# Four of 32 row tiles get their vector added by TensorE instead of VectorE, two inverse roots go to GpSimd, thirteen instead of fourteen places for x, and a new order of the work

## The chip, the cores and the metric

The kernel runs on one core of one Trainium2 chip. The metric is the device time of one execution in microseconds (us): the median of three runs of the kernel before is 146.02 us (145.58 to 146.04). Engines are named as in the profile: PE is TensorE, DVE is VectorE, ACT is ScalarE, POOL is GpSimd, SP is SyncE, which here only issues DMAs. Sequences carry a q (SPq, ACTq): the time in which such an engine issues a DMA.

## The reference

x has 8 sequences of 512 rows of 1024 float32 values, 16 MB. Each sequence is cut into 8 blocks of rows, and one vector p per sequence is made from them and added to all its rows; what follows is a layer norm and a residual.

```python
block_repr = inputs.reshape(B, 8, block_size, H).sum(axis=2)
keys = einsum('bnh,kh->bnk', block_repr, Wk)
keys = keys / sqrt(mean(keys * keys, -1) + EPS) * rms_weight
attn = softmax(einsum('bnh,h->bn', keys, cond[1]))
attended = einsum('bn,bnh->bh', attn, block_repr)
p = einsum('bsh,kh->bsk', attended, Wo)       # the same for all rows of a sequence
y = x + p
out = x + (y - mean(y)) / sqrt(var(y) + EPS) * ln_gamma + ln_beta
```

## The kernel before

**Tiles and groups.** The 8 sequences are three groups of 2, 4 and 2 sequences (`GROUPS`). A "row" is a tile of 128 partitions by 1024 values; there are 32 rows, 0 to 7 in group 0, 8 to 23 in group 1, 24 to 31 in group 2. A load of 1 MB brings two rows: x0.0 is rows 0 and 1, x1.2 is rows 12 and 13, x1.3 rows 14 and 15, x2.3 rows 30 and 31. Loaded tiles live in 14 places of SBUF (`XSLOTS`), in which the 8 MB of the two weight matrices also stand before they are transposed. A result is written over its row in place, stored from there, and only then can the place take another load.

**A group's p.** PE sums the blocks (bs, L429), DVE turns the sums into columns (col, L439), PE multiplies by Wk (proj.0, L473), then comes the softmax: ACT squares (L496), DVE sums keys by q (qk, L498), PE collects both (L505), DVE forms the mean square cv (L507), and an inverse root of it is made by `inverse_root`: ACT takes logarithm and exponential (L484, L485), and three small steps n1, n2, n3 on DVE or POOL (L486 to L489) refine it. After scores, maximum, exponential (L513) and sum (wc, L516), PE multiplies by Wo (proj.1), DVE or ACT weighs that (vw, L529 or L530), PE spreads it over 128 partitions (L545), and two copies make `pb`, p of the group in SBUF. Four small DMAs (tb, L387) put p's rows into a table `tab` that also holds gamma and beta.

**A row k** is worked on in five steps, whose labels are used below:

- S_k (DVE, L646): x = x + p in place, with the row's sum beside it
- Q_k (ACT, L648): the sum of squares around the mean
- D_k (DVE, L746): (gamma + std) * x into a pair of PSUM banks
- R_k (PE, L732): outer products that add what depends on the row's statistics, for two rows in one go
- E_k (ACT, L761): PSUM times 1 / std back into the row, which is then stored (L813)

Rows form units of 2 or 4 (`UNITS`); a unit's statistics are worked on by POOL (s2, v, std, sd2, rs; std and rs are powers of 0.5 and -0.5, L695 and L715), transposed by PE (L721) and copied out of PSUM (lt, L241 on ACT or L243 on DVE). D, R and E share three pairs of PSUM banks, so D of a row waits for E of a row three places earlier.

**The order** is written out by hand: `Plan` collects the steps with what they read and write, and `ORDER` lists their numbers in the order in which they are given to the engines (with the bank or place that a step takes, and a letter for the engine where there is a choice). Each engine works through its own part of that list strictly in order. Words such as `f1:7` are matmuls with zeros, which open a bank for accumulation and keep PE at work.

`UKIND` names the way of each unit. In kind `c` the steps are as above. Kind `p`, which is in the code before but used by no unit, leaves x as it is: B_k sums the row, Bp sums p (both independent of each other), POOL adds the two sums (`totals`), Y_k on PE adds x (times an identity) and p in PSUM, and Q_k squares from there. Its outer products then take p * gamma from a second table, `tabx`.

## Time and profile before

| | us |
|---|---|
| median of three runs | 146.02 |
| time of the profiled execution | 144.9 |
| its span, first to last instruction | 143.2 |
| DVE busy in the span | 95.5 |
| ACT busy | 90.9 |
| PE busy (zeros among it) | 112.3 |
| POOL busy | 58.5 |

The second part of the page cuts the span in 40 slices. DMA is at 9 tenths or more in slices 1 to 15, up to about 57 us: the loads of the weights and of most of x. From slice 20 on DVE shows 9 in nearly each slice, and ACT 8 or 9: there the rows are worked on. Of 42.76 MB, 25.73 are read and 16.78 written; 1 MB of a load takes some 2.5 us when the DMA engines are full. The granted clock of TensorE is 0.932 on average.

### The profile page before, as it was taken

Reading aid. Unit: us, or ns where it says so; the run is one execution under the profiler, and the core shown is the slowest. Engines: PE = TensorE matmul, PEld = TensorE weight load, DVE = VectorE, ACT = ScalarE, POOL = GpSimd, SP = SyncE. Lnnn points to the kernel's source line nnn. Section 1 sums busy time; section 2 is a strip of 40 time slices with the busy share of each in tenths; the row PEclk is TensorE's granted clock in tenths of the full one; section 3 lists DMA queues with packets and bytes.
Section 4 is the critical chain, followed back from the end, with each engine's and each line's share of the span. In section 5 each row is a group of like instructions: output and inputs, shape, how many; then the busy total and the mean of one; then the engine's idle time right before and its main releaser. Section 6 shows DMA issues by size and latency. Waiting matters only on the chain.

```text
span 143.2 us, 2871 instructions
## 1 busy us (share of the span) xinstructions
PE 112.3 (78%) x1093; PEld 58.9 (41%) x1101; DVE 95.5 (67%) x161; ACT 90.9 (64%) x140; POOL 58.5 (41%) x107
## 2 busy tenths in 40 slices
...
GB/s 126 427 413 422 413 409 414 410 411 423 426 410 424 410 413 420 263 0 238 204 307 417 314 295 5 293 89 204 291 298 6 347 240 0 295 293 220 411 401 145
DMA packets 7526, 42.76 MB, mean 299 GB/s; under 512 B 808, under 2 KB 808, under 8 KB 3672
## 3 DMA queue, kind: packets, MB, share of 16 engines
...
HBM read 25.73 MB, written 16.78 MB: 297 GB/s over the span
## 4 chain that ended last, share of the span: by engine, by line
DMA 33%; PE 24%; DVE 17%; ACT 11%; issue 6%; POOL 3%; SPq 2%; DVEq 0%; ACTq 0%
PE b L473 11%; DVE t L746 9%; DMA gam<-in_L_cond_ln_gamma_dram 8%; DMA x<-in_L_cond_Wo_dram 8%; DMA x<-in_L_cond_Wk_dram 6%; DMA x<-in_x_dram 5%; PE t L732 5%; PE t L407 4%; ACT x L761 4%; DVE x L646 4%; ACT square L648 3%; DMA tab<-in_L_cond_ln_gamma_dram 3%; DMA pb<-in_cond_dram 3%; ACT woT L241 2%; PE b L429 1%
## 5 line engine op out<-in xcount | busy, mean ns | idle before, releaser
L746 DVE SCALAR_TENSOR_TENSOR t<-gam,ustd,x 128x1024 f32<-128x1024 f32 x31 | 39.1, 1291 | 3.7 <-ACT x L761 2.5
L648 ACT ACTIVATE square<-x,tot 128x1024 bf16<-128x1024 f32 x32 | 36.7, 1147 | 3.3 <-DVE x L646 2.1
L646 DVE SCALAR_TENSOR_TENSOR x<-x,pb 128x1024 f32<-128x1024 f32 x32 | 37.6, 1223 | 0.1
L761 ACT ACTIVATE x<-t,urs 128x1024 f32<-128x1024 f32 x31 | 33.2, 1107 | 5.5 <-PE t L732 2.4
L700 POOL TENSOR_SCALAR stat<-tot 128x8 f32<-128x8 f32 (+1 forms) x8 | 7.5, 934 | 53.1 <-DVE x L646 53.0
L732 PE MATMUL t<-tab,lt 32*128 32x512 f32 x124 | 24.9, 667 | 4.8 <-DVE lt L243 2.2
L407 PE MATMUL t<-ident,x 128*128 128x128 f32 x120 | 17.9, 316 | 5.3 <-DMA x<-in_L_cond_Wk_dram 3.0
L869 PE MATMUL b<-zeros 128*128 128x512 bf16 (+1 forms) x57 | 18.2, 439 | 2.1 <-DVE zeros L294 1.0
L407 PEld LDWEIGHTS t<-ident,x 128*128 128x128 f32 x120 | 16.9, 202 | 6.6 <-issue 4.7
L869 PEld LDWEIGHTS <-zeros 128*128 128x128 bf16 x87 | 8.7, 108 | 17.2 <-issue 12.8
L695 POOL TENSOR_TENSOR ustd<-uv,halfs 128x4 f32<-128x4 f32 (+1 forms) x8 | 13.3, 1660 | 5.5 <-DVE uv L692 4.1
L732 PEld LDWEIGHTS t<-tab,lt 32*128 32x128 f32 x124 | 7.5, 191 | 16.9 <-DVE t L746 5.7
L241 ACT COPY wkT<-t 128x1024 f32<-128x1024 f32 x5 | 5.1, 1013 | 14.1 <-PE t L407 14.1
L715 POOL TENSOR_TENSOR urs<-uv,halfs 128x4 f32<-128x4 f32 (+1 forms) x8 | 13.2, 1650 | 0.0
L243 DVE COPY wkT<-t 128x1024 f32<-128x1024 f32 x3 | 3.7, 1225 | 12.1 <-PE t L407 12.1
L429 PE MATMUL b<-x,blk 128*32 128x256 f32 x128 | 8.4, 384 | 4.2 <-DMA x<-in_x_dram 3.7
L473 PE MATMUL b<-wkT,blkT 128*32 128x256 f32 x192 | 11.0, 380 | 0.6 <-DVE blkT L439 0.6
L241 ACT COPY woT<-t 128x1024 f32<-128x1024 f32 x6 | 5.8, 1014 | 7.8 <-PE t L407 7.8
L429 PE MATMUL t<-x,blk 128*32 128x256 f32 x128 | 7.9, 382 | 3.1 <-DMA x<-in_x_dram 3.1
L473 PEld LDWEIGHTS b<-wkT,blkT 128*32 128x32 f32 x192 | 5.9, 110 | 5.8 <-issue 1.2
L473 PE MATMUL b<-woT,blkT 128*32 128x256 f32 x128 | 7.9, 382 | 0.0
L869 PE MATMUL t<-zeros 128*128 128x512 bf16 x22 | 6.4, 380 | 1.1 <-ACT lt L241 0.6
...
## 6 DMA issues: line engine op xcount, KB each, us to landing
...
```

Of the source, the lines that this page charges most:

```text
L241: nc.scalar.copy(dst, src)
L407: nc.tensor.transpose(half(part, c // 4)[:, bass.ts(c % 4, P)], tile_of(name)[:, e % RT, c::HC], ident)
L429: nc.tensor.matmul(bank(f"bs{n}")[32 * j : 32 * j + 32, :QU], blk[G["g"]], tile_of(name)[:, r, bass.ts(j, QU)], start=(t == 0 and r == 0), ...
L473: nc.tensor.matmul(bank(name)[32 * j : 32 * j + 32, :QU], b[:, c, :], w[:, c, j], start=(c == 0), stop=(c == HC - 1),)
L646: add(f"S{k}", [(DVE, 1.15)], lambda e: nc.vector.scalar_tensor_tensor(x_row(k), x_row(k), 1.0, pb[n], ALU.mult, ALU.add, accum_out=total) ...
L648: add(f"Q{k}", [(ACT, 1.28)], lambda e: nc.scalar.activation(square, x_row(k), AF.Square, bias=total, scale=-float(H), accum_out=ssq), rea ...
L695: add(f"{T} std", [(POOL, 0.5 + 0.16 * U)], lambda e: nc.gpsimd.tensor_tensor(std, v, halfs[:, :1].to_broadcast([P, U]), ALU.pow), reads=[ ...
L715: add(f"{T} rs", [(POOL, 0.5 + 0.16 * U)], lambda e: nc.gpsimd.tensor_tensor(rs, v, halfs[:, 1:].to_broadcast([P, U]), ALU.pow), reads=[V, ...
L732: nc.tensor.matmul(half(f"row{k}", h), lts[q % NST][lo : lo + 32, r // RT, :], tab_of(k)[0][lo : lo + 32, :], start=False, stop=True, skip ...
L746: add(f"D{k}", [(DVE, 1.21)], lambda e: nc.vector.scalar_tensor_tensor(flat(pair(name)), gam, std, x_row(k), ALU.add, ALU.mult), reads=["g ...
L761: add(f"E{k}", [(ACT, 1.13)], lambda e: nc.scalar.activation(x_row(k), flat(pair(name)), AF.Identity, scale=rs), reads=[RS], writes=[xk(k) ...
L869: nc.tensor.matmul(bank_at(i)[:, :n], zeros, zeros[:, 0:1].to_broadcast([P, n]), start=start, stop=True, skip_group_check=True)
```

## The change

- Unit 3 (rows 12 to 15) becomes kind `p`: S12 to S15 on DVE go; B12, B13 and B14 on DVE and B15 on ACT sum x, Bp1.0 on DVE sums p of group 1, Y12 to Y15 are done on PE, and Q12 to Q15 read PSUM. POOL gets two steps more for the unit (`to`, and `sn`, the unit's constant columns). The table `tabx` (tx1, one DVE product) and the tile `gx` for it (four small loads by ACT) are new.
- In the softmaxes of groups 1 and 2 (`ROOT_POW`) one power on POOL takes the place of logarithm, exponential, n1, n2 and n3.
- The two tables take SBUF, so `XSLOTS` is 13; `diag` and `kw` share the tile `vw0`, and some small tiles that no kind uses are left out. The second to fourth loads of group 2 instead of the third and fourth wait for a stored place.
- `ORDER` is new in all parts. Engines of single steps change with it: the copies lt of units 2, 3, 4 and 7, vw of group 1 and one copy of its pb go from ACT to DVE; the two half scalings of the last row (E31), the copy qw and some copies of transposed weights go from DVE to ACT (one of the latter the other way); the step v of units 7 and 8 leaves DVE for POOL and ACT. 87 matmuls with zeros become 64.

```diff
-XSLOTS = 14
+XSLOTS = 13
-UKIND = 'ccccccccc'
-TABS = ((0, 'y'), (1, 'y'), (2, 'y'))
-FORMS = ('y',)
+UKIND = 'cccpccccc'
+TABS = ((0, 'y'), (1, 'x'), (1, 'y'), (2, 'y'))
+FORMS = ('x', 'y')
+ROOT_POW = (1, 2)
...
-    "42 94b 43 f1:1 119:4 44 45 46 47 72:7 106 48 120a 117:0 49 50 51 52 118a 121:2 53 54 55 56 73:8 102 57 122b "
+    "40 41 42 94a 43 f1:1 124:4 44 45 46 47 72:7 99 48 125a 122:0 49 50 51 52 123b 126:2 53 54 55 56 73:8 102 57 "
...
-    diag = alloc("diag", [P, 32])
+    diag = vw[0][:, :32]
-    kw = alloc("kw", [P, QU], BF16) if junk is None else junk[:, :QU]
+    kw = vw[0]
...
-        inverse_root(T, cv, c0, ca, ca, ("cv", "c0", "ca", "ca"))
+        if n in ROOT_POW:
+            add(f"{T} pow", [(POOL, 2.0)], lambda e: nc.gpsimd.tensor_tensor(
+                ca, cv, halfs[:, 1:].to_broadcast([P, NBLK]), ALU.pow), reads=["cv", "halfs"], writes=["ca"])
+        else:
+            inverse_root(T, cv, c0, ca, ca, ("cv", "c0", "ca", "ca"))
...
-        elif kind_of(k) == "p":
-            add(f"B{k}", [(ACT, 1.28)], lambda e: nc.scalar.activation(square, x_row(k), AF.Identity, accum_out=usx[u][:, r : r + 1]),
+        elif kind_of(k) in "pa":
+            sx = usx[u][:, r : r + 1]
+            add(f"B{k}", [(ACT, 1.34), (DVE, 1.2)], lambda e: nc.scalar.activation(
+                square, x_row(k), AF.Identity, accum_out=sx) if e == ACT else nc.vector.tensor_reduce(sx, x_row(k), AX.X, ALU.add),
                 reads=[xk(k)], writes=[f"usx{u}.{r}"])
...
+            add(f"Bp{n}.0", [(ACT, 1.34), (DVE, 1.2)], lambda e: nc.scalar.activation(
+                square, pb[n % NPB], AF.Identity, accum_out=t[:, 0:1]) if e == ACT else nc.vector.tensor_reduce(
+                t[:, 0:1], pb[n % NPB], AX.X, ALU.add),
```

The step that carries the addition, in the code before and after alike (in `moments`, kind `p`):

```python
for h in range(2):
    nc.tensor.matmul(pair(y)[:, h, :]..., ident, bands(x_row(k))[:, :, h, :], start=True, stop=False)
spread_p(G, y, False)          # four matmuls of 256 columns that add p
```

**First place: DVE around p of group 0.** L516 or L531 is the last small step of the softmax (wc), L530 or L545 is vw, the copy to `pb` ends the making of p, and then the S steps of rows 0 to 7 follow; the whole-row loads of gamma (`gam`) and col of group 1 come behind them. Before:

```order
L515 RECIPROCAL es<-es 128x1
L516 SCALAR_TENSOR_TENSOR kw,wcol<-cs,es,diag_90 128x8
L530 TENSOR_SCALAR vw_107<-t_79,wcol 128x256
L243 COPY pb_108<-b_82 128x4x128
L646 SCALAR_TENSOR_TENSOR x_64,tot_97<-x_64,pb_108 128x1024 x2
```

and now (L617 are B12 and B13, then B14):

```order
L531 SCALAR_TENSOR_TENSOR vw_105,wcol<-cs,es,diag_88 128x8
L617 TENSOR_REDUCE usx_141<-x_65 128x1 x2
L545 TENSOR_SCALAR vw_105<-t_79,wcol 128x256
L617 TENSOR_REDUCE usx_141<-x_66 128x1
L253 COPY pb_106<-b_81 128x4x128
L693 SCALAR_TENSOR_TENSOR x_64,tot_95<-x_64,pb_106 128x1024 x2
```

Two sums of x stand ahead of vw and one ahead of the copy.

**Second place: DVE between p of group 1 and col of group 2.** Before, eight S (rows 8 to 15), D8, D9, col:

```order
L646 SCALAR_TENSOR_TENSOR x_75,tot_97<-x_75,pb_109 128x1024 x2
L646 SCALAR_TENSOR_TENSOR x_76,tot_97<-x_76,pb_109 128x1024 x2
L646 SCALAR_TENSOR_TENSOR x_63,tot_98<-x_63,pb_109 128x1024 x2
L646 SCALAR_TENSOR_TENSOR x_65,tot_98<-x_65,pb_109 128x1024 x2
L746 SCALAR_TENSOR_TENSOR t_81<-gam,ustd_156,x_75 128x1024
L746 SCALAR_TENSOR_TENSOR t_79<-gam,ustd_156,x_75 128x1024
L439 STREAM_TRANSPOSE blkT_105<-b_82 128x256
```

and now four S of rows 8 to 11 with Bp1.0 (L627) among them, D7 behind them, five S of rows 16 to 20, D8, D9, the copy lt of unit 2, tx1 (L401) and col:

```order
L693 SCALAR_TENSOR_TENSOR x_75,tot_95<-x_75,pb_107 128x1024 x2
L627 TENSOR_REDUCE pmv_114<-pb_107 128x1
L693 SCALAR_TENSOR_TENSOR x_63,tot_95<-x_63,pb_107 128x1024 x2
L799 SCALAR_TENSOR_TENSOR t_78<-gam,ustd_143,x_71 128x1024
L693 SCALAR_TENSOR_TENSOR x_68,tot_95<-x_68,pb_107 128x1024 x2
L693 SCALAR_TENSOR_TENSOR x_70,tot_95<-x_70,pb_107 128x1024 x2
L693 SCALAR_TENSOR_TENSOR x_73,tot_96<-x_73,pb_107 128x1024
L799 SCALAR_TENSOR_TENSOR t_78<-gam,ustd_144,x_75 128x1024
L799 SCALAR_TENSOR_TENSOR t_80<-gam,ustd_144,x_75 128x1024
L253 COPY lt_101<-b_82 128x256
L401 TENSOR_TENSOR tabx<-tab_109,gx 128x512
L449 STREAM_TRANSPOSE blkT_103<-b_81 128x256
```

D7 was ahead of the first S of this group, and later rows' S have moved up into the place of S12 to S15.

**Third place: PE behind p of group 1.** Before, it does two block sums of group 2, R of rows 6 and 7, and the third block sum:

```order
L545 MATMUL b_83<-vw_107,spread_94 128x4x64
L869 LDWEIGHTS zeros
L869 MATMUL t_79<-zeros 128x512
L429 MATMUL b_82<-x_72,blk_91 32x256 x8
L429 MATMUL b_82<-x_74,blk_91 32x256 x8
L732 MATMUL t_79<-tab_110,lt_104 128x512 x2
L732 MATMUL t_80<-tab_110,lt_104 128x512 x2
L429 MATMUL b_82<-x_64,blk_91 32x256 x8
```

and now Y14 and Y12 (each L657 and the four L560 behind it) come first, Y15 and Y13 behind R of rows 6 and 7, and the last two block sums of group 2 after those:

```order
L657 MATMUL t_78<-x_66,ident 128x512 x2
L560 MATMUL t_78<-vw_105,spread_92 128x4x64 x4
L657 MATMUL t_80<-x_65,ident 128x512 x2
L560 MATMUL t_80<-vw_105,spread_92 128x4x64 x4
L439 MATMUL b_81<-x_74,blk_89 32x256 x8
L439 MATMUL b_81<-x_64,blk_89 32x256 x8
L785 MATMUL t_79<-tab_108,lt_102 128x512 x2
L785 MATMUL t_78<-tab_108,lt_102 128x512 x2
L657 MATMUL t_80<-x_66,ident 128x512 x2
L560 MATMUL t_80<-vw_105,spread_92 128x4x64 x4
L657 MATMUL t_79<-x_65,ident 128x512 x2
L560 MATMUL t_79<-vw_105,spread_92 128x4x64 x4
```

Behind the last row follow the transposes of unit 2, two block sums and R of rows 8 and 9. The Y steps use the pairs of banks that D, R and E share.

## Rows read from the trace of the kernel before

**Rows 1.** Windows: length; busy PE, PEld, DVE, ACT, POOL; PE clock; DMA share, GB/s.

```profile
56.14:73.64 17.50, 15.72 (x191) 7.29 (x194) 12.88 (x23) 9.97 (x20) 5.31 (x5) 1.00 0.54 200
73.64:106.62 32.98, 28.20 (x271) 12.44 (x265) 32.46 (x54) 30.64 (x49) 17.58 (x17) 0.95 0.62 252
79.00:85.00 6.00, 5.42 (x38) 1.82 (x29) 6.00 (x10) 5.55 (x9) 5.28 (x6) 0.72 0.82 327
```

**Rows 2.** Timeline of DVE, 40 to 58 us: start, length, instruction [idle before].

```profile
40.32 0.23 DVE L516 SCALAR_TENSOR_TENSOR kw<-cs,es,diag 128x8 bf16<-128x8 f32 x1
...
43.06 0.48 DVE L530 TENSOR_SCALAR vw<-t,wcol 128x256 f32<-128x256 f32 x1 [2.51 <-PE t L459]
...
45.74 1.23 DVE L646 SCALAR_TENSOR_TENSOR x<-x,pb 128x1024 f32<-128x1024 f32 x1
...
56.14 0.69 DVE L352 TENSOR_SCALAR gam<-gam 128x1024 f32<-128x1024 f32 x1 [1.10 <-DMA gam<-in_L_cond_ln_gamma_dram]
...
57.11 1.25 DVE L746 SCALAR_TENSOR_TENSOR t<-gam,ustd,x 128x1024 f32<-128x1024 f32 x1
```

**Rows 3.** Timeline of PE, 39 to 55 us.

```profile
39.30 3.70 PE L459 MATMUL t<-woT,blkT 128*32 128x192 f32 x128
...
52.36 1.07 PE L429 MATMUL t<-x,blk 128*32 128x256 f32 x16 [0.66 <-DMA x<-in_x_dram]
...
54.88 0.42 PE L429 MATMUL t<-x,blk 128*32 128x256 f32 x4 [1.13 <-DMA x<-in_x_dram]
```

**Rows 4.** Timelines of DVE, 65 to 74 us, and ACT, 72 to 74 us.

```profile
65.39 0.16 DVE L507 TENSOR_SCALAR cv<-b 128x8 f32<-128x8 f32 x1
...
67.31 0.17 DVE L489 SCALAR_TENSOR_TENSOR ca<-ca,c 128x8 f32<-128x8 f32 x1
...
72.44 1.29 DVE L746 SCALAR_TENSOR_TENSOR t<-gam,ustd,x 128x1024 f32<-128x1024 f32 x1 [0.89 <-ACT x L761]
73.64 1.22 DVE L646 SCALAR_TENSOR_TENSOR x<-x,pb 128x1024 f32<-128x1024 f32 x1
...
72.30 1.06 ACT L241 COPY pb<-b 128x512 f32<-128x512 f32 x2
```

**Rows 5.** Timeline of DVE, 111 to 117 us.

```profile
111.85 1.22 DVE L646 SCALAR_TENSOR_TENSOR x<-x,pb 128x1024 f32<-128x1024 f32 x1
...
113.00 3.69 DVE L746 SCALAR_TENSOR_TENSOR t<-gam,ustd,x 128x1024 f32<-128x1024 f32 x3
116.58 1.22 DVE L646 SCALAR_TENSOR_TENSOR x<-x,pb 128x1024 f32<-128x1024 f32 x1
```

**Rows 6.** Groups of instructions by line: busy us, mean ns, idle before.

```profile
L243 DVE COPY lt<-b 128x256 f32<-128x256 f32 x2 | 0.8, 422 | 0.0
```

**Rows 7.** Timeline of PE, 58 to 80 us.

```profile
58.20 3.66 PE L473 MATMUL b<-wkT,blkT 128*32 128x256 f32 x64
...
78.43 1.07 PE L429 MATMUL b<-x,blk 128*32 128x256 f32 x16 [2.49 <-DMA x<-in_x_dram]
```

**Rows 8.** Timeline of POOL, 52 to 53 and 110 to 112 us.

```profile
52.54 1.04 POOL L695 TENSOR_TENSOR ustd<-uv,halfs 128x4 f32<-128x4 f32 x1 [0.88 <-ACT uv L691]
...
110.92 1.91 POOL L695 TENSOR_TENSOR ustd<-uv,halfs 128x4 f32<-128x4 f32 x1
```

**Rows 9.** Timeline of ACT, 74 to 77 us.

```profile
74.90 1.15 ACT L648 ACTIVATE square<-x,tot 128x1024 bf16<-128x1024 f32 x1 [0.52 <-DVE x L646]
...
76.17 1.15 ACT L648 ACTIVATE square<-x,tot 128x1024 bf16<-128x1024 f32 x1
```

**Rows 10.** Timelines of DVE, ACT and SP, 134 to 139 us.

```profile
134.36 1.42 DVE L771 SCALAR_TENSOR_TENSOR b<-gam,ustd,x 128x512 f32<-128x512 f32 x2
136.33 1.41 DVE L780 TENSOR_SCALAR x<-b,urs 128x512 f32<-128x512 f32 x2 [0.55 <-PE b L732]
...
135.98 1.11 ACT L761 ACTIVATE x<-t,urs 128x1024 f32<-128x1024 f32 x1 [0.37 <-PE t L732]
...
137.55 1.38 SPq L807 DMA_DIRECT2D out_dram<-x  x2
```

More of the change, by code (lines that the diff above doesn't have):

```diff
@@ L32 @@
 UP = 32768.0
+ADD_ISSUE = 1.3
+BY_PE = ()
+ROOT_POW = (1, 2)
+DIVIDE = False
+ADD_MB = 2.0
 SINGLE = (28, 29, 30)
@@ L231, in block_attn_resid_kernel @@
     ussq, uv, u0, ua, urs, usx, ustd = (
-        [alloc(f"{n}{i}", [P, MAXU]) for i in range(NU)] for n in ("ussq", "uv", "u0", "ua", "urs", "usx", "ustd")
+        [alloc(f"{n}{i}", [P, MAXU]) for i in range(k)] * (NU // k) if k else [None] * NU for n, k in (
+            ("ussq", NU), ("uv", NU), ("u0", 1), ("ua", NU if "b" in UKIND else 1), ("urs", NU),
+            ("usx", NU if set(UKIND) & set("pa") else 0), ("ustd", NU))
     )
@@ L388, in table @@
                 out=t[32 * q + 2 : 32 * q + 2 + g, :], in_=p[0:P:w, i * HALF : (i + 1) * HALF]),
-                reads=[f"pb{n % 2}.{j}" for j in range(2)], writes=[f"tab{n % NTAB}.{q}"], mb=0.01)
+                reads=[f"pb{n % NPB}.{j}" for j in range(2)], writes=[f"tab{n % NTAB}.{q}"], mb=0.01)
         if (n, "x") in TABS:
@@ L464, in project @@
                     add(f"{name}.{at}.{c0}.{qs}.{cs}", [(PE, 0.012 * cs + 0.108 * qs * cs)], lambda e, go=go: go(),
-                        reads=[f"blkT{n % 2}"] + w_keys(which, range(2 * at, 2 * (at + qs)), halves[0]),
+                        reads=[f"blkT{n % NBT}"] + w_keys(which, range(2 * at, 2 * (at + qs)), halves[0]),
                         claim=("b", name) if at == c0 == 0 else None, use=[] if at == c0 == 0 else [name])
@@ L477, in project @@
             add(f"{name}.{c0}", [(PE, 0.98)], lambda e, go=go: go(),
-                reads=[f"blkT{n % 2}"] + w_keys(which),
+                reads=[f"blkT{n % NBT}"] + w_keys(which),
                 claim=None if c0 else ("b", name), use=[name] if c0 else [])
```

100 lines of the change are left out of this document (66 added, 34 removed), and 41 rows, old and new, of the table ORDER.

## Prediction

> **What bounds the kernel now.** I read the page's slices first, then the windows by stage, then the timelines of DVE, PE and ACT along the chain that ended last. Up to 57 us the loads set the pace: the last block sums of group 1 start 2.52 us apart, each when its tile lands [rows 3], and DVE has gaps. From 73.64 us on DVE sets it: in a stretch of 32.98 us it is busy for 32.46, with ACT close behind at 30.64 and PE at 28.20, zeros included [rows 1]. In the stage between, 17.50 us long, DVE works 12.88: there the softmax of group 1 and the first D, R, E form one chain. So a microsecond of DVE work is worth a microsecond after 73.64 us only as long as ACT (E, Q) and PE (R) give the banks back in time, and before 57 us it is worth what the next load does not hide.
>
> Prices, as starts to next starts: S 1.15 (111.85 to 113.00), D 1.19 (three in 3.58) [rows 5], Q 1.27 (74.90 to 76.17, [rows 9]), E 1.05 to 1.11 [rows 10]; a copy lt on DVE 0.36 to 0.42 [rows 6].
>
> **Loads' stage: B12 to B15 and p of group 0.** Tiles land 2.5 us apart; counting back from 52.36 (x1.6, [rows 3]), x1.2 lands at about 42.3 and x1.3 at 44.8. DVE has wc done at 40.55 and before waited 2.51 us for vw [rows 2]. Now B12 and B13 stand in that gap, but can't start before 42.3. The trace has no whole-row sum without an addition; it lies between the 0.69 of the one-input gamma step [rows 2] and the 1.15 of S. I take 1.15, since S reads the row once too and gives a sum. So vw starts at 44.6 instead of 43.06; a block sum now ahead of proj.1 on PE (3.70 us from 39.30, [rows 3]) makes that end near 44.1, so PE is not what it waits for. From vw to S0 it took 2.68 us (43.06 to 45.74), in which B14 and, on ACT, B15 fit. S0 starts about 1.5 late, at 47.3. Eight S end at 56.5; before, DVE sat 1.10 us waiting for gamma until 56.14 [rows 2], and that cover absorbs most: col, gamma, D0 at 57.4 to 57.5 instead of 57.11. Cost 0.35, between 0 (sums at 0.69: vw at 43.7, S over before gamma lands) and 1.0 (x1.3 or B14 late).
>
> **Middle stage.** For group 1 the power on POOL replaces five steps on three engines; from cv to the root they took 2.1 us (65.39 to 67.48, [rows 4]), with D4 among them. Four columns of power take 1.04 alone and 1.91 right behind another step [rows 8]; eight lie between 1.04 and 3.8 (twice 1.91), and I take 1.8, near the rows. That is nothing on the chain, where D4 must be over too; what it saves are small steps on DVE and ACT. Both copies of pb were made one after the other by ACT in 1.06 [rows 4], now they stand on two engines: 0.5 sooner. With the 0.35 carried in and vw on DVE at the same price as on ACT, p is there about 0.3 sooner than the 73.36 of before, and D7, which stood ahead of S8 (72.44), has moved behind: S8 at 72.6 with 1.19 of D7 owed, 73.8 against 73.64. Cost 0.15, bounds -1 and +1.
>
> **Rows' stage, DVE's sum.** S12 to S15 go: -4.6. Bp1.0 comes: +1.15 (0.69 to 1.15). tx1 comes: 512 columns, +0.55 (0.35, half of gamma's step, to 0.71, half of the last D in [rows 10]). Four copies lt come: three at 0.36 and a half-sized one, +1.3. n2, n3 of softmax 2 and v of units 7 and 8 go: four steps of 0.1 to 0.2, -0.5. Sum -2.1, bounds -2.8 and -1.9.
>
> **Rows' stage, what takes it back.** A Y on PE is two matmuls of 512 columns through all 128 rows and four of 256 of which two run side by side. The 64 records of proj.1.0 are 8 rounds of 256 columns in 3.66 us, 0.4575 a round [rows 7]; a Y is 2 + 2 + 2 rounds, 2.75 us. The bounds are 2.3 (weight loads and rounds overlap better) and 3.5 (about 0.2 more for each of four loads of weights that no side-by-side round hides). Four Y are 11 us in a stretch in which PE has 32.98 - 28.20 = 4.8 us free and does zeros besides, so they fit, but not in any order. Replaying the queue: p's spread ends at 71.9 (S8's 72.6 less a copy); Y14 to 74.7, Y12 to 77.4; two block sums (1.07) to 79.5, the second waiting as before for a load (78.43, [rows 7]); R of rows 6 and 7 waits for D7. D7 needs the bank that Q14 frees; ACT does E5, Q8, Q9, then Q14 once Bp and POOL's sum are there, to 78.6, so D7 is 78.6 to 79.8 and R ends at 81.0. Y15 needs the bank of Q12 (81.1) and ends at 83.9, Y13 at 86.6, unit 2's transpose at 87.0, the last block sums at 89.1, R of rows 8 and 9 at 90.2. DVE meanwhile does 9 S, Bp, D7, D8, D9, lt, tx1 and reaches col at 88.75: 0.35 of waiting. Behind it ACT is the tight one: E8 at 90.9, and from there its list of E and Q leaves DVE 0.5 waiting ahead of D15 and 0.6 ahead of S24 (ACT makes one half of p behind Q23, E14, E15, Q22). That is 1.45, against 0.5 of idle time that DVE had in this stretch before, of which I let 0.15 stay: +1.1, bounds 0 and 4.
>
> **Places and loads.** x2.3 now waits for the third stored tile. By the replay it is asked for at about 80, when the store of rows 4 and 5 is over, and lands near 85 (two transfers of 2.5); its block sum stands behind Y13 and is due at 88. Nothing, with 3 us of cover; without that cover a late landing counts in full.
>
> **Shared interfaces.** The S at 111.85, beside a power on POOL (110.92 to 112.83), took 1.22 us, and the S at 73.64, where POOL has nothing to do by its timeline, 1.22 too [rows 4, 5, 8]: a power beside DVE costs DVE nothing here, and POOL's additional work, some 5 us (two powers of 1.8, `sn` and `to`), enters the sum with 0. The Trainium skill, GPSIMD Engine Reference, Key points, says that GpSimd shares its SBUF interfaces with VectorE and contends with its instructions that have two SBUF inputs, as S and D have. By that rule this change, which puts more on POOL, would lengthen DVE; the two S speak against it.
>
> **The end.** E31 goes from DVE (136.33, 1.41) to ACT, where it stands behind E30 (135.98 to 137.09) and takes two halves of 0.55 to 0.7: 138.2 instead of 137.74. But the last issue of SP started some 0.35 behind its data anyway (two issues, 1.38, from 137.55 [rows 10]). +0.15, bounds 0 and +0.7.
>
> **Sum.** +0.15 - 2.1 + 1.1 + 0.15 = -0.7. The profiled execution took 144.9 with a span of 143.2, so 1.7 lie around it, untouched; it would take 144.2. The median of the runs, 146.02, is 1.1 above that execution; I put the same difference on it: 145.3.
>
> **Rivals.**
> 1. DVE's sum counts in full. The waits are like before's and B12 to B14 cost nothing: -2.1, 143.9. For it: col needs only a Y some 0.15 shorter, and the granted clock, 0.72 from 79 to 85 us [rows 1] behind a wait of 2.49 us on a load, has no such wait left ahead of it. Against it: ACT, busy 30.64 of 32.98, loses little more than 2 us in that stretch.
> 2. No change: ACT sets the pace. DVE's busy time falls as summed, but ACT keeps all its Q and E, and DVE waits for banks: 146.0. For it: ACT's small reserve. Against it: five small copies leave ACT.
> 3. Slower: Y on PE. R of rows 8 and 9 and col of group 2 stand behind Y15 and Y13 in one queue, and Y15 behind R of rows 6 and 7. With e more per Y, R8 ends 2e later, and 2e - 0.45 more once the slack ahead of D7 is used. At e = 0.3 (Y of 3.05) the gain is gone; at 0.55 (3.3) it is +1.75 - 0.7 = +1.05, 147.1; with half the clock there, as 0.72 shows for part of it, Y15 and Y13 alone add 5.5: near 150. For it: no row here has a matmul with 128 rows and 512 columns in float32. Against it: 0.4575 a round is from 64 records in a row.
> 4. POOL holds DVE up, as weighed above: 5 us more of POOL work, paid by S and D that stand still: +5 - 0.7, 150.3. Only the two equal S bear on it, and they are against it.
>
> **How the numbers follow.** The forecast (145.3, own range 144.6 to 146.0) has 0.45, rival 1 0.17, rival 2 0.15, rival 3 0.20, rival 4 0.03. About 0.3%, 0.44 us, is what can be told from no change, that is 145.6 to 146.5. Faster: 0.33 of the forecast, all of rival 1, 0.02 of rival 2: 0.52. Same: 0.11 of the forecast, 0.11 of rival 2, 0.01 of rival 3: 0.23. Slower: the rest, 0.25. The range from 143.6 to 147.5 takes in rival 1 with a little for cheaper sums of x, and rival 3 up to a Y of some 3.4; left out are the half clock, rival 4 and a gain above 2.4.
>
> **What would show it.** Right: vw of group 0 near 44.6 and D0 near 57.4; S8 near 72.6 with D7 behind four S; Y of 2.7 to 2.8; col of group 2 near 89 with DVE idle ahead of it for under 1 us; DVE's busy time 3 to 4 us lower than 95.5 plus the sums B12 to B14. Wrong: a Y over 3 us or a low clock between 79 and 90; DVE idle for more than 2 us in all behind 73 us because of E; a power of eight columns over 2.5 us with the score step waiting; S longer where POOL works; or a landing of x2.3 behind 88 us.

## The result, and the profile after

The change made the kernel slower: 147.53 us (median of 20 runs) against 145.25 us of before, ratio 1.0123 with a 95% interval of 1.010 to 1.0146. The ratio is taken over the 18 of 20 executions of each kernel in which no die ran slower, so it is less than the quotient of the two medians, and the loss is 1.8 us by it. Forecast were 145.3 and "faster". The forecast took off 0.7 from a median of three runs, 146.02; by the median of 20, before takes 145.25 itself. The profiled execution of after took 147.99 with a span of 146.1, that of before 144.9, so this pair of profiles, 3.1 us apart, shows the loss larger than it is.

Windows of after (length; busy PE, PEld, DVE, ACT, POOL; clock; DMA), cut from D0 to S8, from S8 to S24 (the last window of [rows 1] ends earlier, ahead of S23), from there to the end of D31, and a part of the last stage:

```profile
58.11:73.55 15.44, 13.99 (x168) 6.32 (x169) 11.56 (x20) 8.54 (x16) 6.73 (x6) 1.00 0.36 133
73.55:109.80 36.25, 35.29 (x309) 15.56 (x309) 33.66 (x52) 31.81 (x49) 20.49 (x21) 1.00 0.64 254
109.80:138.86 29.06, 23.89 (x88) 7.80 (x90) 26.78 (x38) 24.50 (x34) 14.39 (x14) 0.85 0.59 240
122.00:130.00 8.00, 6.84 (x22) 2.04 (x21) 7.21 (x11) 6.23 (x10) 7.65 (x8) 0.57 0.64 263
```

In the second stretch DVE is idle for 36.25 - 33.66 = 2.59; before it was 0.52 in [rows 1], and still 0.52 when that window is carried on to S24 (73.64 to 109.56, DVE busy for 35.40). So DVE works 1.7 us less on the same work and waits 2.1 more. PE is now the fullest engine there. In the last stage DVE is idle for 2.28, and the clock is half for most of 122 to 130.

The same work, then, at four points. D0 starts at 58.11 (57.11, [rows 2]): +1.0. When D19 is done and S24 next, 111.08 (S24 at 109.89, with D19's 1.19 still owed) stands against 109.56: +1.5. D31 ends at 138.86 against 135.78: +3.1. From there to the end it is 7.24 against 7.42. So 1.0 was lost by D0, 0.5 in the rows' stage, in which 1.2 should have been gained, and 1.6 in the last stage, of which the prediction had said nothing but +0.15. All these are sums of the one pair of profiles.

**p of group 0.** Timeline of DVE (start, length, instruction, idle before), answering [rows 2]:

```profile
41.34 0.23 DVE L531 SCALAR_TENSOR_TENSOR vw<-cs,es,diag 128x8 f32<-128x8 f32 x1
42.50 2.35 DVE L617 TENSOR_REDUCE usx<-x 128x1 f32<-128x1024 f32 x2 [0.93 <-DMA x<-in_x_dram]
45.01 0.48 DVE L545 TENSOR_SCALAR vw<-t,wcol 128x256 f32<-128x256 f32 x1 [0.17 <-PE t L469]
...
47.75 1.23 DVE L693 SCALAR_TENSOR_TENSOR x<-x,pb 128x1024 f32<-128x1024 f32 x1
...
57.35 0.64 DVE L362 TENSOR_SCALAR gam<-gam 128x1024 f32<-128x1024 f32 x1
58.11 1.29 DVE L799 SCALAR_TENSOR_TENSOR t<-gam,ustd,x 128x1024 f32<-128x1024 f32 x1
```

B12 starts when x1.2 lands and vw stands behind B13, as forecast. The wait for gamma is gone: its cover is used up, and what is late at S0 is late at D0.

**The crunch behind p of group 1.** POOL, ACT, DVE and PE of after:

```profile
65.01 2.60 POOL L520 TENSOR_TENSOR ca<-cv,halfs 128x8 f32<-128x8 f32 x1 [1.95 <-DVE cv L517]
...
77.16 2.22 POOL L708 TENSOR_SCALAR tot<-usx,pmv 128x4 f32<-128x4 f32 x1 [6.87 <-DVE pmv L627]
```

```profile
79.42 1.11 ACT L661 ACTIVATE square<-t,tot 128x1024 bf16<-128x1024 f32 x1 [2.09 <-POOL tot L708]
```

```profile
67.65 0.17 DVE L524 SCALAR_TENSOR_TENSOR cs<-b,ca 128x8 f32<-128x8 f32 x1 [0.32 <-POOL ca L520]
...
78.11 1.22 DVE L693 SCALAR_TENSOR_TENSOR x<-x,pb 128x1024 f32<-128x1024 f32 x1
...
80.66 1.29 DVE L799 SCALAR_TENSOR_TENSOR t<-gam,ustd,x 128x1024 f32<-128x1024 f32 x1 [1.32 <-ACT square L661]
...
91.52 0.45 DVE L449 STREAM_TRANSPOSE blkT<-b 128x256 f32<-128x256 f32 x1 [0.52 <-PE b L439]
```

```profile
72.92 1.98 PE L657 MATMUL t<-x,ident 128*128 128x512 f32 x4 [0.20 <-ACT x L814]
74.84 1.14 PE L560 MATMUL t<-vw,spread 64*128 64x256 f32 x8
```

Read the rows as one chain: POOL adds four columns in 2.22; ACT, strictly in order, waits 2.09 for that with Q14 at the head of its queue; D7 waits 1.32 for the bank that Q14 frees; col comes at 91.52 (85.19 before, when it stood earlier in the work; 89.1 was forecast). A Y takes 2.98 (72.92 to the next step, 75.90).

**The last stage.** PE, DVE and ACT:

```profile
126.76 2.09 PE L785 MATMUL t<-tab,lt 32*128 32x512 f32 x8 [0.23 <-DVE lt L253]
...
130.42 2.16 PE L785 MATMUL t<-tab,lt 32*128 32x512 f32 x8
```

```profile
130.11 1.29 DVE L799 SCALAR_TENSOR_TENSOR t<-gam,ustd,x 128x1024 f32<-128x1024 f32 x1 [0.87 <-ACT x L814]
...
133.81 1.29 DVE L799 SCALAR_TENSOR_TENSOR t<-gam,ustd,x 128x1024 f32<-128x1024 f32 x1 [1.01 <-ACT x L814]
```

```profile
140.11 1.12 ACT L814 ACTIVATE x<-t,urs 128x1024 f32<-128x1024 f32 x1 [2.67 <-PE t L785]
```

R of rows 24 and 25 takes 2.09 at half the clock where R of two rows takes 1.14 at the full one, E24 follows late, and D27, the D at 130.11, waits 0.87 for its bank. D28 at 131.51 has no wait; D29 at 133.81 waits 1.01. R of rows 26 and 27, at 130.42, takes 2.16 although the clock is full again: it waits for D27 between its halves. At the end E30 waits 2.67 for R30. Before has one such wait in this stage already, ahead of its D28:

```profile
129.84 2.55 DVE L746 SCALAR_TENSOR_TENSOR t<-gam,ustd,x 128x1024 f32<-128x1024 f32 x2 [0.77 <-ACT u L484]
```

So of the 1.6 lost in this stage 0.87 is D27's wait, 0.24 what D29's wait has over that of before, and the rest a little more work of DVE and short gaps.

### The profile page after: what moved, and what is told of

Same layout as the page of the kernel before. It is cut to its first block, busy times and chain, and to the rows that moved or that the text cites. A ratio compares the mean times of both kernels' runs of the same rounds, so it can differ in the third digit from the quotient of the medians.

```text
span 146.1 us, 2914 instructions
## 1 busy us (share of the span) xinstructions
PE 122.7 (84%) x1119; PEld 61.4 (42%) x1126; DVE 96.3 (66%) x155; ACT 92.1 (63%) x138; POOL 60.8 (42%) x109
## 4 chain that ended last, share of the span: by engine, by line
PE 36%; DVE 22%; DMA 16%; POOL 9%; issue 8%; ACT 5%; POOLq 1%; ACTq 0%; DVEq 0%
DVE x L693 10%; PE b L483 10%; DMA x<-in_L_cond_Wo_dram 8%; DVE t L799 7%; PE t L417 6%; DMA x<-in_L_cond_Wk_dram 5%; PE t L785 5%; DMA pb<-n_L_cond_rms_weight_dram 3%; PE t L657 3%; PE b L439 3%; POOL ustd L747 2%; PE t L469 2%; ACT x L814 2%; ACT square L695 2%; POOL urs L768 2%
## 5 line engine op out<-in xcount | busy, mean ns | idle before, releaser
L695 ACT ACTIVATE square<-x,tot 128x1024 bf16<-128x1024 f32 x28 | 32.1, 1146 | 3.3 <-DVE x L693 1.9
L693 DVE SCALAR_TENSOR_TENSOR x<-x,pb 128x1024 f32<-128x1024 f32 x28 | 33.0, 1221 | 0.3
L753 POOL TENSOR_SCALAR stat<-tot 128x8 f32<-128x8 f32 (+1 forms) x8 | 5.0, 624 | 40.7 <-DVE x L693 40.6
L922 PE MATMUL b<-zeros 128*128 128x512 bf16 x47 | 16.6, 479 | 2.2 <-DVE zeros L304 1.0
L251 ACT COPY wkT<-t 128x1024 f32<-128x1024 f32 x4 | 4.0, 1012 | 14.8 <-PE t L417 14.8
L922 PEld LDWEIGHTS <-zeros 128*128 128x128 bf16 x64 | 6.2, 111 | 16.2 <-issue 13.0
L253 DVE COPY wkT<-t 128x1024 f32<-128x1024 f32 x4 | 4.9, 1224 | 12.1 <-PE t L417 12.1
L785 PEld LDWEIGHTS t<-tab,lt 32*128 32x128 f32 x108 | 6.5, 196 | 15.2 <-DVE t L799 7.5
L747 POOL TENSOR_TENSOR ustd<-uv,halfs 128x4 f32<-128x4 f32 (+1 forms) x8 | 10.8, 1346 | 1.3 <-ACT uv L743 0.9
L657 PE MATMUL t<-x,ident 128*128 128x512 f32 x16 | 7.9, 618 | 0.3 <-ACT x L814 0.2
```

The costliest lines, as they stand in the source:

```text
L657: nc.tensor.matmul(pair(y)[:, h, :].rearrange("p (q d) -> p q d", d=P), ident, bands(x_row(k))[:, :, h, :], start=True, stop=False, skip_g ...
L693: add(f"S{k}", [(DVE, 1.15)], lambda e: nc.vector.scalar_tensor_tensor(x_row(k), x_row(k), 1.0, pb[n], ALU.mult, ALU.add, accum_out=total) ...
L695: add(f"Q{k}", [(ACT, 1.28)], lambda e: nc.scalar.activation(square, x_row(k), AF.Square, bias=total, scale=-float(H), accum_out=ssq), rea ...
L747: add(f"{T} std", [(POOL, 0.5 + 0.16 * U)], lambda e: nc.gpsimd.tensor_tensor(std, v, halfs[:, :1].to_broadcast([P, U]), ALU.pow), reads=[ ...
L785: nc.tensor.matmul(half(f"row{k}", h), lts[q % NST][lo : lo + 32, r // RT, :], tab_of(k)[0][lo : lo + 32, :], start=False, stop=True, skip ...
L922: nc.tensor.matmul(bank_at(i)[:, :n], zeros, zeros[:, 0:1].to_broadcast([P, n]), start=start, stop=True, skip_group_check=True)
```

## The experiments

Theory: the rows on PE do save DVE its 2 us, but (W) POOL's `to` holds up ACT and D7, (E) the sums ahead of p of group 0 use up gamma's cover, (H) PE's clock falls on R24, and (P) the power of 8 columns is dearer than the steps it replaces. Rivals: PE's queue of Y's sets the pace by itself (Y), or the store queue at the end hides all of it (D). All ratios are to the kernel before, run together with each of them; the changed kernel has 1.0123. Compare ratios from row to row, not medians. 1 point of a ratio, 0.01, is 1.45 us.

| kernel | median us | ratio | 95% interval |
|---|---|---|---|
| e1, the power alone in before | 146.68 | 1.0083 | 1.0045 to 1.0121 |
| e2, Bp1.0 ahead of S8 | 145.80 | 1.0013 | 0.9979 to 1.0047 |
| e3, B12 to B14 later | 146.40 | 1.0051 | 1.0018 to 1.0083 |
| e4, four zeros more | 146.18 | 1.0032 | 0.9997 to 1.0067 |
| e5, all reliefs | 144.13 | 0.9932 | 0.9897 to 0.9966 |
| e6, e2 and E31 on DVE | 146.46 | 1.0056 | 1.0021 to 1.0091 |
| e7, e2 and the old roots | 147.60 | 1.0146 | 1.0094 to 1.0197 |
| e8, e5 with PE busier | 144.03 | 0.9896 | 0.9846 to 0.9946 |
| e9, before with PE busier | 146.12 | 1.0036 | 1.0003 to 1.0068 |
| e10, `to` on DVE | 146.66 | 1.0046 | 1.0007 to 1.0085 |
| e11, after with PE busier only | 146.49 | 1.0048 | 1.0015 to 1.0080 |
| e12, e8 with D7 early | 143.52 | 0.9878 | 0.9852 to 0.9903 |

### W: POOL in ACT's way (e2, e10)

e2, DVE's queue by labels (ACT's and POOL's are as they were):

```diff
 p1 cp0
+Bp1.0
 S8
 S9
-Bp1.0
 S10
```

> The changed kernel with one step moved: Bp1.0, DVE's sum of p, stands ahead of S8 instead of behind S9. POOL's sum `to` (2.22 us) then runs from about 74.8 to 77.0 while ACT does Q8 and Q9, and Q14 starts at about 77.4 instead of 79.42. Theory W (ACT's wait for POOL is what the crunch pays for): ACT's idle 2.09 and DVE's 1.32 go, col of group 2 comes 1.0 to 1.3 sooner, time 1.0 to 1.3 less than the changed kernel's 147.5: 146.2 to 146.5. Rival Y (PE's queue of Y15, Y13, block sums and R8 sets col's time, the wait is hidden by it): under 0.4 gained, col still at 91 or later, 147.1 to 147.5.

POOL, ACT and DVE of e2:

```profile
74.45 2.22 POOL L707 TENSOR_SCALAR tot<-usx,pmv 128x4 f32<-128x4 f32 x1 [4.58 <-DVE pmv L626]
```

```profile
78.18 1.11 ACT L660 ACTIVATE square<-t,tot 128x1024 bf16<-128x1024 f32 x1
```

```profile
79.42 1.29 DVE L798 SCALAR_TENSOR_TENSOR t<-gam,ustd,x 128x1024 f32<-128x1024 f32 x1 [0.49 <-ACT square L660]
...
90.28 0.45 DVE L448 STREAM_TRANSPOSE blkT<-b 128x256 f32<-128x256 f32 x1 [0.52 <-PE b L438]
```

`to` still takes 2.22, but now beside Q8 and Q9, and ACT's wait for it is gone. Not all of ACT's waiting is: with Bp ahead of S8, ACT waits 1.61 for S8 instead of 0.41, and D7 still waits 0.49. Col comes 0.9 sooner than in e4 and e11 (91.24 and 91.20), whose D0 is within 0.15 of the one here. The ratio fell by 1.1 points, some 1.6 us, more than W's 1.0 to 1.3 and far from rival Y's 0.4. But in the profiled execution of e2 the half clock of PE fell on 117 to 121, and D27 doesn't wait; up to 0.87 of the 1.6 can be that wait, which is another matter (H below).

e10 leaves Bp1.0 where it was and gives `to` to DVE:

```diff
-            add(f"U{q} to", [(POOL, 0.5)], lambda e: nc.gpsimd.tensor_scalar(
+            add(f"U{q} to", [(POOL, 0.5), (DVE, 0.2)], lambda e: engine[e].tensor_scalar(
```

> The changed kernel with one step on another engine: `to` (the total of x plus that of p, 4 columns) on DVE behind S10 instead of on POOL, Bp1.0 where it was. Theory W (2.22 of POOL in ACT's way is what the crunch pays for): `to` takes under 0.3 on DVE, Q14 starts near 78.4 instead of 79.4, col near 90.4, time 0.8 to 1.3 less than the changed kernel, ratio 1.000 to 1.005. Rival B (it is Bp's place in DVE's queue, not POOL): col less than 0.4 sooner, ratio 1.009 or more.

DVE of e10:

```profile
77.89 0.23 DVE L707 TENSOR_SCALAR tot<-usx,pmv 128x4 f32<-128x4 f32 x1
...
79.47 1.29 DVE L798 SCALAR_TENSOR_TENSOR t<-gam,ustd,x 128x1024 f32<-128x1024 f32 x1 [0.22 <-ACT square L660]
...
90.32 0.45 DVE L448 STREAM_TRANSPOSE blkT<-b 128x256 f32<-128x256 f32 x1 [0.52 <-PE b L438]
```

The same four columns take 0.23 on DVE, and col is at 90.32, as in e2. Two different cures of one wait give the same col and ratios whose intervals overlap: the wait for POOL is shown as a cause, at 0.9 by col. The ratios give 1.1 to 1.6, but in the profiled execution of e10, too, D27 has no wait, so they may hold a part of the clock's loss. The Trainium skill, GPSIMD Engine Reference, 3.1 Elementwise, puts GpSimd at 1.96 times VectorE's time for a long two-input operation and names two software dispatches for each instruction; on four columns the rows here show 2.22 against 0.23, so the long operation's ratio is no price for a small one.

### E: the sums ahead of p of group 0 (e3)

```diff
 sm0 wc
-B12
-B13
 v0 w
-B14
 p0 cp0
...
 D2
+B12
 sm1 qk
 sm1 sdd
+B13
...
 sm1 mx
+B14
```

On PE the first block sum of group 1 went back behind proj.1, the second behind p's spread.

> The changed kernel with the first p as before: B12, B13, B14 leave the way to p of group 0 (B12 goes behind D2, B13 behind sdd, B14 behind mx, where DVE stood idle for 1.04, 1.22 and 0.83), the first block sum of group 1 goes back behind proj.1, the second behind p's spread. Theory E (the sums ahead of p cost about 1.0 because they use up the cover by the landing of gamma): S0 back near 45.8, D0 near 57.1, of which B14 gives back up to 0.4: 0.6 to 1.0 less than the changed kernel, 146.5 to 146.9. Rival C (the 1.0 is a low clock on PE in this one execution, from the block sum at 28.5 on): D0 moves by less than 0.3 and the time by less than 0.3.

DVE of e3:

```profile
46.71 1.22 DVE L692 SCALAR_TENSOR_TENSOR x<-x,pb 128x1024 f32<-128x1024 f32 x1 [0.42 <-ACT pb L250]
...
57.29 3.79 DVE L798 SCALAR_TENSOR_TENSOR t<-gam,ustd,x 128x1024 f32<-128x1024 f32 x3
```

D0 is at 57.29, where e2, e4, e10 and e11, which leave these sums in the way, have 57.68 to 57.88. So the sums cost 0.4 to 0.6. Why the profiled execution of after is another 0.2 to 0.4 later is not shown: its softmax ended at 41.34 (39.2 to 40.4 in all of these), but its B12 waited for x1.2 all the same. S0 came at 46.71, not at 45.8, since B15 now stood ahead of ACT's copy of p. The ratio fell by 0.7 points, 1.05 us, in E's range of 0.6 to 1.0 within the noise. That is more than the sums account for: col, at 90.93, is only 0.3 sooner than in e4 and e11. In the profile D27 waits 0.37 instead of 0.87, and two block sums moved on PE as well.

### H: PE's clock in the last stage (e4, e11, e9, e6)

e4 puts four matmuls on zeros ahead of the transpose of unit 6; e11 does that and also fills PE's two gaps of 1.09 inside R of rows 20, 21 and of rows 22, 23:

```diff
-f6:7 R20
+f6:7 R20 f4:7 R21
...
-f6:7 R22
+f6:7 R22 f4:7 R23
...
-f1:6 U6_mm
+f1:6 f4:6 U6_mm
```

> The changed kernel with four more matmuls on zeros ahead of the transpose of unit 6 (PE stood idle there from 123.2 to 124.1, and the granted clock fell to 0.50 from 123 to 130). Theory H (R of rows 24 and 26 at half the clock make E late and DVE wait 0.87 and 1.01): clock 1.00 from 120 to 135, those waits gone, 1.0 to 1.6 less than the changed kernel, 145.9 to 146.5. Rival N (the clock of the last stage falls in some executions and not in others, whatever stands there, or costs nothing in the median): within 0.4 of the changed kernel, 147.1 to 147.9.

> The changed kernel with nothing but PE kept busier ahead of R24: R of rows 20 and 21, and of 22 and 23, row by row with four matmuls on zeros between, and four ahead of the transpose of unit 6. Theory H (of the changed kernel's loss, what lies behind 110 is the half clock on R24 and R26): col of group 2 stays near 91.3, clock 1.00 from 112 to 134, waits of 0.87 and 1.01 ahead of D28 and D29 down to under 0.5, ratio 1.000 to 1.005 instead of 1.0123. Rival W (the crunch alone is the loss, the clock costs nothing in most executions): ratio 1.009 or more.

Windows of e4, then of e11:

```profile
122.00:130.00 8.00, 7.29 (x30) 2.44 (x28) 7.96 (x12) 7.18 (x11) 7.68 (x8) 0.79 0.64 263
```

```profile
122.00:130.00 8.00, 5.90 (x30) 1.95 (x28) 7.96 (x12) 7.17 (x11) 7.68 (x8) 1.00 0.65 265
130.00:136.00 6.00, 4.96 (x22) 1.46 (x19) 4.73 (x10) 5.59 (x9) 1.88 (x2) 1.00 0.69 285
136.00:144.00 8.00, 3.51 (x9) 1.15 (x8) 1.58 (x3) 2.45 (x4) 0.00 (x0) 0.50 0.78 311
```

Read by the queue's order, the wait of 0.87 that both expectations put ahead of D28 is D27's. In e4 the ratio fell by 0.9 points to 1.0032, as H said of the time, but not by H's way: the clock still fell, to 0.51 in 122 to 124 and 0.63 in 124 to 126. It fell there instead of on R24, R24 ran at the full clock, and D27's wait is gone.

In e11 the clock is full from 70 to 136, D27 no longer waits either, col is at 91.20, so nothing of the crunch changed, and 0.75 points are won with work that computes nothing. Two cures of D27's wait, one that moves the half clock and one that holds it off, give ratios that agree: the half clock on R24 is shown as a cause. Over the executions counted the mean granted clock is 0.954 to 0.974 in e11 and 0.921 to 0.966 in after; among those of after it doesn't sort the times. Half of the expectation failed: D29's wait (1.02) stayed in both, so that one is the order of E's and not the clock, and the half clock came anyway, at the end, where E30 waits 2.67 as in after. The Trainium skill, TensorE: Matmul & The Clock Gate, section What's actually happening, says that half the clock is the default and PE's activity releases it; e11 agrees for the stretch that it fills. When the clock falls also differs between executions of nearly the same queue: 0.83 was the mean from 112 to 122 and 1.00 from 122 to 130 in e2, against 0.99 and 0.59 in e6.

e9 is the kernel before with more zeros.

```diff
-f3:7 U5_mm
+f3:7 f5:7 U5_mm
...
-U6_mm f5:6
+f5:6 U6_mm f5:6
...
-R24
+f3:6 R24
...
-f4:7 R28
+f4:7 f3:7 R28
```

> The kernel before, in its own order, with more matmuls on zeros in the last stage alone: five ahead of the transposes of units 5 and 6 each, three more ahead of R24 and of R28. It is the control for the clock: does the gain come from the rows on PE or from PE's clock, which would help the kernel before too? Theory S (before is not held up by the clock: its dip at 112 to 117 lies where E waits 0.48 only): within 0.4 of before, ratio 0.997 to 1.003. Rival H (the clock's dip costs before about 1 as well): ratio 0.990 to 0.995, as low as the kernel with all the reliefs.

DVE of e9, D27:

```profile
128.50 1.29 DVE L747 SCALAR_TENSOR_TENSOR t<-gam,ustd,x 128x1024 f32<-128x1024 f32 x1 [0.74 <-ACT x L762]
```

It gained nothing: 1.0036, a little above S's 0.997 to 1.003 and far from H's 0.990 to 0.995. As a control it falls short, since the clock wasn't full: in its profile the stretch below full clock only moved, from 113 to 117 in before to about 120 to 126, and D27 now waits 0.74, which it doesn't in before. So zeros in these places don't help before; what a full clock would give it was not tried. That its own stretch of half clock costs it little rests on its trace, where DVE doesn't wait behind it.

e6 took E31 back to DVE on top of e2:

```diff
-E30 R31.1 E31.1a st30 E31.0a
+E30 R31.1 E31.0b E31.1b st30
```

> The kernel with Bp1.0 ahead of S8 (145.8, ratio 1.0013 to before) and beside that only the two halves of E31 on DVE, as before, instead of ACT behind E30. Theory T (E31 on ACT costs the end what the prediction gave it or more): last computation 0.4 to 0.6 sooner and time 0.2 to 0.6 less, 145.2 to 145.6. Rival D (the queue of stores sets the end): last computation sooner, time within 0.2 of 145.8.

The expected gain is not there, and no loss can be told either: its interval overlaps that of e2, and its profile had the half clock on R24, with a wait of 0.86 ahead of D27, which that of e2 had not. What E31's engine is worth stays open, below what these runs resolve.

### P: the power of 8 columns (e1, e7)

e1 is the kernel before with `ROOT_POW = (1, 2)` and nothing else of the change:

```diff
-sm2 ln   sm2 ex   sm2 n1   sm2 n2   sm2 n3
+sm2 pow
```

> One part alone: the kernel before, in its own order, with 14 places and S12 to S15 on DVE, but with the two roots of softmax 1 and 2 as one power of GpSimd in place of their five steps. In the trace after the change the power of 8 columns took 2.60 and 2.53 us and the score step behind it waited 0.32 and 0.31. Theory P (the power costs): slower than before by 0.3 to 0.7, 145.6 to 146.0. Rival K (rows 12 to 15 on PE cost all of it, and the power saves five small steps): 0 to 0.5 faster, 144.8 to 145.3.

POOL and DVE of e1:

```profile
95.79 2.57 POOL L519 TENSOR_TENSOR ca<-cv,halfs 128x8 f32<-128x8 f32 x1
98.44 1.19 POOL L743 TENSOR_SCALAR uv<-ussq 128x4 f32<-128x4 f32 x1
99.72 1.94 POOL L746 TENSOR_TENSOR ustd<-uv,halfs 128x4 f32<-128x4 f32 x1
```

```profile
101.69 1.29 DVE L798 SCALAR_TENSOR_TENSOR t<-gam,ustd,x 128x1024 f32<-128x1024 f32 x1 [0.63 <-POOL ustd L746]
```

The power costs before 0.8%, 1.2 us (0.45 to 1.21%), and the 146.68 lies above P's 145.6 to 146.0. What shows in the profile is less the score step than what is queued behind the power: std of unit 4 ends 1.3 later than in before, and D16 waits 0.63 for it (e7's expectation names it D17).

e7 puts the old roots into e2's order:

```diff
-sm2 pow
+E12  sm2 ln  sm2 ex (ACT)   sm2 n1 (POOL)   sm2 n2  sm2 n3 (DVE)
```

> The kernel with Bp1.0 ahead of S8 (145.8) and beside that both softmax roots as before: ln and exp on ACT, one step on POOL, two on DVE, no power of 8 columns. The power alone in the kernel before cost 0.8% (0.45 to 1.2). Theory P (POOL's 2.5 us power holds up POOL's queue or the score step in this order too): waits 0.32 and 0.31 ahead of the score steps gone, 0.4 to 1.0 less, 144.8 to 145.4. Rival O (the cost of the power in the kernel before comes from its place in that order, where U4's std stood behind it and D17 waited 0.63; here it doesn't): no less than 145.6, and up to 146.4 since ten small steps come back on DVE and ACT.

DVE of e7:

```profile
102.42 0.17 DVE L497 SCALAR_TENSOR_TENSOR ca<-ca,cv 128x8 f32<-128x8 f32 x1 [1.22 <-POOL ca L496]
```

A miss for P and, at 147.60, for rival O's 145.6 to 146.4 too: 1.3% or 1.9 us slower than e2. Behind E12 the logarithm comes late on a full ACT, and DVE waits 1.22 instead of 0.31, which is 0.9 of it. About as much again is the clock: it was 0.50 from 124 to 128, and D27 waited 0.86, where e2's profile has no such wait. So the power has no price of its own that holds everywhere. In the order of before it delays POOL's queue; in the new order, with ACT full, it is the shorter way by some 0.9. Other places for ln and exp were not tried.

### Together, and what bounds it then (e5, e8, e12)

e5 has Bp1.0 first, the sums of x in idle time (B14 on ACT), e4's zeros, unit 6's lt ahead of D25, E31 on DVE, one zero less ahead of R30:

```diff
 D24
+U6 lt
 D25
-U6 lt
...
-f1:7 R30
+R30
```

> The changed kernel with all the reliefs together: Bp1.0 ahead of S8; the first block sum of group 1 behind proj.1, B12 behind D2 and B13 behind sdd on DVE, B14 on ACT ahead of E2 (idle there for 2.07), B15 behind ACT's copy of p; four zeros ahead of the transpose of unit 6, one less ahead of R of row 30; the copy lt of unit 6 ahead of D25; the halves of E31 on DVE. Theory A (the delays stand one behind the other on one chain, as e2, e3, e4 each took off 0.7 to 1.1%): D0 near 57.2, D7 and col 1.0 sooner than in e2 (col near 89.5 or earlier), no wait of DVE over 0.5 behind 105, time 144.0 to 144.9, less than before. Rival D (the stores set the end: they ran at 0.85 to 1.03 of the DMA engines' time from 134 us on): what is gained before 134 doesn't show, 145.0 to 145.8.

Faster than before (0.9932), as A said; col is at 90.00, not at 89.5, and D29 still waits 0.82. In the profiled execution (145.76) the clock was half behind 135, and taking the zero from ahead of R30 was an error: the bank of D31 was then opened behind R30, and D31's second half waited 1.79. e8 mends that and fills PE's gaps as e11 does:

```diff
-U8_mm E28 U8_lt E29 R30
+U8_mm f3:6 E28 U8_lt E29 f1:7 R30
```

> The kernel with all the reliefs (e5: 144.1, ratio 0.9932; its times lay in two groups, 143.6 to 144.1 and 145.8 to 147.1, and in the profiled execution of 145.76 the clock was 0.50 from 122 to 125 and from 135 on), with PE kept busier: R of rows 20 and 21, and of 22 and 23, issued row by row with four matmuls on zeros between (PE stood idle there for 1.09 each), three zeros behind the transpose of unit 8, and the one ahead of R of row 30 put back. Theory H (idle time of PE ahead of R24 lets the clock fall there, and that makes the slower group): clock 1.00 from 112 to 134, no wait over 0.4 of DVE between 105 and 131, median 143.5 to 144.1 and few times over 145. Rival N (the clock falls once in the last 35 us wherever that comes): a dip of as many us elsewhere, as many times in the slower group, 144.0 to 145.5.

Windows of e8:

```profile
122.00:130.00 8.00, 7.00 (x30) 2.22 (x29) 7.96 (x12) 7.79 (x13) 7.03 (x8) 1.00 0.69 282
130.00:136.00 6.00, 5.72 (x25) 2.25 (x26) 4.87 (x10) 4.04 (x6) 1.20 (x1) 1.00 0.76 313
```

Full clock up to 136, 0.34 left of D29's wait, five of six times at or under 144.41. e12 then lets D7 start as early as it can:

```diff
 S8
+U3 to (DVE)
 S9
 S10
+D7
 S11
-D7
...
 Q8
+Q14
 Q9
-Q14
```

> The kernel with all the reliefs and the busier PE (e8, ratio 0.9896), and in the crunch `to` on DVE behind S8, Q14 ahead of Q9, and D7 ahead of S11: D7 some 1.4 sooner, near 77.6. In e8 PE ran from 72.1 to 92 with no gap (four Y of 2.97, four block sums, R6, the transpose). Theory Y (PE's queue now sets col of group 2, the third rival of the prediction): col stays within 0.2 of 89.87 although D7 is early, time within 0.3 of e8, 143.7 to 144.3. Rival A (ACT and D7 set it): col 0.5 to 1.0 sooner, 143.0 to 143.5.

DVE and PE of e12:

```profile
77.65 1.29 DVE L800 SCALAR_TENSOR_TENSOR t<-gam,ustd,x 128x1024 f32<-128x1024 f32 x1 [0.18 <-ACT square L662]
...
89.78 0.45 DVE L450 STREAM_TRANSPOSE blkT<-b 128x256 f32<-128x256 f32 x1 [0.20 <-PE b L440]
```

```profile
81.45 1.98 PE L658 MATMUL t<-x,ident 128*128 128x512 f32 x4 [0.44 <-ACT square L662]
83.37 1.13 PE L561 MATMUL t<-vw,spread 64*128 64x256 f32 x8
84.43 1.98 PE L658 MATMUL t<-x,ident 128*128 128x512 f32 x4
86.34 1.14 PE L561 MATMUL t<-vw,spread 64*128 64x256 f32 x8
87.41 0.44 PE L775 MATMUL b<-ident,stat 128*128 128x128 f32 x2
87.78 1.93 PE L440 MATMUL b<-x,blk 128*32 128x256 f32 x32
```

D7 is 1.36 sooner than in e8 (79.01), col 0.09 sooner (89.87): theory Y by col. By time it can't be told: 143.52 is just below Y's 143.7 to 144.3, and the ratio is 0.2 points under e8's, within the intervals. PE does not set col alone either: Y15 at 81.45 waits 0.44 for ACT's Q12, and from there PE runs without a gap to col, where DVE arrives 0.20 earlier. ACT's list of Q's and then PE's queue stand one behind the other, and an earlier D7 gains nothing there. e12, at 0.9878, has the lowest ratio of these kernels. How much of that the reliefs alone would give the kernel before, without rows on PE, was not tried, except for the zeros (e9); nor was the new order without rows on PE.

## Why the prediction was wrong, point by point

The step that failed is the time given to POOL's sum `to` under "what takes it back": taken as well under 1 us, it measured 2.22, and ACT and D7 waited for it. A second loss, the half clock on R24, lies in the last stage, which the sum took over unchanged.

- **Loads' stage, +0.35.** Mechanism right (B12 at the landing, cover used up), size within its bounds: 0.4 to 0.6 by e3 and its neighbours. The row sum takes 1.17 (1.15 was taken), and S0 came at 47.3 to 47.5 in e2, e4 and e11, as forecast.
- **Middle stage, power of 1.8 "nothing on the chain".** It took 2.60 and 2.53 and the score steps waited 0.32 and 0.31. The bound (3.8) held it, the value taken was too small. The rule behind that value, a power alone takes 1.04 and one right behind another step 1.91, doesn't hold: four columns took 1.00 right behind another step (102.69 in after). That S8 comes at 72.6 failed (73.55).
- **DVE's sum, -2.1.** -1.7, just outside its bounds (-2.8 to -1.9), though the terms came nearly as priced: Bp 1.13, tx1 0.68 (0.55 was taken), lt 0.34 to 0.41 each. The lt of unit 7 and v of units 7 and 8 stand behind S24 and don't belong to this stage.
- **What takes it back, +1.1: the step that failed.** Idle time of DVE in the stage rose by 2.07 instead of 1.1. The replay let Q14 end at 78.6 "once Bp and POOL's sum are there" and so gave `to` well under 1; the rows of POOL that it had are powers [rows 8]. `to` took 2.22, Q14 ended at 80.6, D7 was 2.06 late: 0.95 of that came in with S8, and about 1.2 is `to` (D7 is at 79.42 and 79.47 in e2 and e10). e2 and e10, without the wait for POOL, have col 0.9 sooner. The trace of before had steps that add to a few columns, and they disagree:

```profile
78.46 1.08 POOL L700 TENSOR_SCALAR stat<-tot 128x8 f32<-128x8 f32 x1 [11.46 <-DVE x L646]
98.07 0.23 POOL L692 TENSOR_SCALAR uv<-ussq 128x4 f32<-128x4 f32 x1 [0.93 <-ACT square L648]
```

The idle time ahead doesn't sort them, and no such row of before has 2.22. What does is how DVE's S and D stand beside them: the first of these steps ends 0.10 behind the end of an S, the second 0.04 behind the end of a D, and `to`, which starts during S10, 0.05 behind the end of S11 (78.11, above). When DVE was idle, two such steps took 0.44 in after:

```profile
79.47 0.44 POOL L753 TENSOR_SCALAR stat<-tot 128x8 f32<-128x8 f32 x2
```

So it looks as if POOL's step is held up by S and D, and not the other way round. That is read from rows; no run tests it by itself.
- **Y, 2.75.** 2.98, inside 2.3 to 3.5; by the third rival's rule (gain gone at 3.05) that alone is less than 0.5. That the extra comes from loads of weights, as the upper bound had it, no run shows. The third rival's 147.1 is near the time by luck: it asks for a Y of 3.3, and e2 and e10 move col without touching a Y. PE's queue is a limit, together with ACT's Q12, once `to` is out of the way (e12).
- **The last stage and the end, +0.15.** Not worked out at all: the sum took the stage as before's, and in the new order the half clock fell on R24, so that D27 waited 0.87. The number of zeros doesn't explain it, for behind R18 there are 27 against 29; their places differ. e11, full clock there and nothing else changed, gives back 0.75 points, about 1.1 us.
- **The rivals.** 1 and 2 fell with the time. Rival 4 fell: the S at 78.11 stands beside POOL's `to` and takes 1.22, like those of before [rows 5].
- **x2.3.** No cost, as said: PE waited for no load ahead of the last block sums.

By their ratios the three losses (e2 or e10, e3, e4 or e11) add up to more than the whole excess of 1.23% over before, since they overlap: e2, e10 and e3 hold a part of D27's wait. By the rows alone they are 0.9 (col), 0.4 to 0.6 (D0) and 0.87 (D27), 2.2 to 2.4 us. With all three taken away the kernel is 0.7 to 1.2% faster than before, 1.0 to 1.8 us; but e5, e8 and e12 have other changes as well (lt of unit 6 sooner, E31 on DVE, in e8 and e12 more zeros, and D29's wait down to 0.34 and 0.33 there), so how much of it is the rows on PE and how much the order is not separated.
